# The causal mask of an LSTM moved from a minimum on VectorE into PSUM products, in a kernel of four attention and expert layers

## The chip, the cores and the metric

The kernel runs on one core of one Trainium2 chip. The metric is the device time of one execution in microseconds (us), the median over several executions. Engines are named as in the profile: PE is TensorE (matrix products; PEld its weight loads), DVE is VectorE, ACT is ScalarE, POOL is GpSimd, and SP is SyncE, which here only issues transfers. PSUM is the memory into which PE writes its results; the kernel divides it into eight banks of 128 x 512 floats. All data is 32-bit float.

## The reference

Eight sequences of 128 tokens of width 128 run through four layers; each is a kind of attention or recurrence followed by a feed-forward stage with routed experts:

```python
x = x + _L0_xattn_ref(_layernorm(x), ctx, ...)          # attention, heads mixed before and after softmax
x = x + _L0_ffn_ref(_layernorm(x), ...)                 # 8 experts, top 2
x = x + _L1_xattn_ref(_layernorm(x), ctx, ctx, ...)     # the LSTM: 8 heads of 16
x = x + _L1_ffn_ref(_layernorm(x), ...)                 # self-attention, then 8 experts, top 1
x = x + _L2_xattn_ref(...); x = x + _L2_ffn_ref(...)    # cross-attention; 8 experts, top 2, one shared
x = x + _L3_xattn_ref(...); x = x + _L3_ffn_ref(...)    # cross-attention; 7 experts, top 1, one shared
```

The change concerns the LSTM of layer 1, whose heads are computed in matrix form:

```python
log_fg = jax.nn.log_sigmoid(fg)
cs = concatenate([zeros((1, 1)), cumsum(log_fg, axis=0)], axis=0)
log_fg_matrix = jnp.where(ltr, (cs - cs.T)[1:, 1:], -jnp.inf)    # ltr: lower triangle
log_D = log_fg_matrix + ig.T
max_log_D = jnp.max(log_D, axis=-1, keepdims=True)
D = jnp.exp(log_D - max_log_D)
C = q @ (k.T / sqrt(DH)) * D
normalizer = jnp.maximum(jnp.abs(C.sum(-1, keepdims=True)), jnp.exp(-max_log_D))
return C / (normalizer + EPS) @ v
```

## The kernel before

**Recording and planning.** The program isn't written in the order in which it runs. The layers are walked through with recording engines (`Noting`, `Engine`): each call makes an operation in a `Plan`, with what it reads and writes. `Plan.schedule` (line 317) then places all 3556 operations on the engines by estimated durations of its own, gives every tile a buffer out of a fixed number for each size (`SLOTS`, line 106; PSUM's eight banks are the class `ps`), and `emit` issues the calls in the order found. Every instruction recorded in this way has the same line in the profile, 486, so groups are told apart by their tiles' names: `ps` is PSUM, `f` a buffer of 1024 columns, `d` of 512, `k` of 256, `h` of 128, `s` of 16, `cst` the constants.

Which operation goes first where several are ready is decided by a due time (`ranks`, line 297): the PE time recorded ahead of the operation in its lane, less the length of the chain that hangs on it, plus a number out of the list `MOVED` (one for each twelve operations in the order of recording, 297 of them). The sequences are treated in two halves of four, each half a lane; lane 1 begins `LAG` later than lane 0 (80e3 ns). An operation that two engines can do (`either`, `on_sbuf`) goes where the plan has it done first: copies out of PSUM on ACT or DVE, elementwise work on SBUF on DVE or POOL.

**The layers.** `first` to `fourth` (lines 1697 to 1728) are walked for each half in turn. Each ends with experts: `route` picks a token's experts and scatters its row into a table in DRAM (`routed_z`); `table` counts the rows of each expert (one product, `cnt`); `run` loads the rows back, transposes them (`zp`), takes the up and down products and stores the results (`routed_y`); the next layer's `combine` gathers these, adds them to the sequence, normalizes and goes on. So each half has, at each layer, two passages through DRAM in which it can't go on, and the other half's work is to fill PE meanwhile.

**The LSTM.** `second` (line 1706) combines layer 0's experts, enters each sequence, and computes the gates of four sequences together (`gates`, line 1474): products for the forget gate (`fp`) and the input gate (`ip`), logarithms and exponentials on ACT, running sums and maxima on DVE, out of which come two arrays `a` and `g`, made so that one product over the 32 rows of a pair of heads gives log D minus its maximum. `self.done` is the last operation of that. Then `heads` (line 1515) is called for each sequence, followed by that sequence's self-attention (`m1`):

- `gm` and `qm` (names `k` in the profile) are made from `g` and the normalized input, on DVE or POOL.
- Eight products over 32 rows each (lines 1530 to 1539) put log D for two heads into columns 0 to 255 of four banks, and q times k into columns 256 to 511.
- On DVE, for each bank, a minimum with the constant `causal` (0 on and below the diagonal of a sequence, -1e30 above it) goes into the SBUF tile `dm` (an `f` buffer), and ACT takes the exponential there, in place (lines 1541 to 1546).
- On DVE, a multiply with the bank's other 256 columns (line 1548).
- Eight products with the values, of 32 columns each (`lav`), a copy, three transposes (`hp`), and the normalizer on DVE and POOL.

A record of PE is one pass: a product of floats makes two records, a transpose one. `plan.gate(op)` (line 229) makes the next operation wait for `op`; `cut()` ends a group of products that are placed together.

Of the kernel before, what the change touches and what calls it, by code (L numbers as in the profile page):

```python
# [14 lines left out]
AF = mybir.ActivationFunctionType  # L15
ALU = mybir.AluOpType
# [59 lines left out]
TURN, START = 93.0, 20.0  # L76
WIRE, LANDED = 290.0, 1350.0
QUEUED = 3700.0
LAG, TAIL = 80e3, 1.0
WEIGHT = {"DVE": 2.0, "ACT": 1.0, "POOL": 1.0}  # L80

TWELVE = 12
MOVED = [
    -1083, -1103, 205, -26, 57, -1175, -1600, -534, 34, -1891, -1239, -1364, -627, -3743,
    -3852, -3408, -603, -286, 235, -1161, 144, -256, 89, -549, -189, -1327, -3092, 41, -483,
    141, -137, -208, -1657, -152, -932, -2161, -2352, -3148, -3024, -2046, -1584, -3502,
    -5867, -1561, -1719, -125, -35, -250, -563, -188, -355, -215, 323, 839, 446, -81, -67,
    -47, 334, 122, 86, -324, 369, 291, -2385, -631, -411, -389, 462, 551, 633, 36, -1330, 187,
    -94, 126, 885, 2267, 2293, 1164, 721, 298, 429, 830, -217, 343, -1869, -623, -2263, -2314,
    -2361, -2571, -2185, -2458, 410, 730, -870, -2137, -615, -230, -384, 1568, 492, 212,  # L90
    -1062, 420, -250, -172, 191, 825, 1849, 456, 1310, -1102, 1348, 1994, -369, -1270, -1096,
    -1627, 75, 108, -498, 90, 936, 32, 25, 1018, 3277, 726, -1256, 3162, -2159, -3746, -1331,
    -490, -407, 130, -1177, 9, 932, 115, 119, -1157, 64, -116, -1259, 80, 3, -316, -1507, -4,
    354, -263, 104, 1161, -594, -1648, -2533, 257, -731, 60, 678, 770, 1063, 81, -220, -934,
    798, 1927, -2080, -2719, -606, 103, 475, -861, -1176, -203, 698, 1199, -4415, -2711,
    -2001, -1291, -638, -375, 1467, -850, 140, -426, 526, -13, -482, -612, -549, 1735, -687,
    -388, -248, 485, -1085, 327, -196, -1695, -57, -534, -652, -881, -1067, 89, 309, 906,
    -1478, -1495, 772, -1075, 279, -312, -853, -1024, -1330, -810, -2709, -4, -804, -2785,
    -2274, -1909, 332, 647, -382, 1390, -41, 1307, -3, -902, 646, 2147, 1652, 2969, 2877,
    1837, 27, 71, -806, -885, 555, -375, 475, 942, 642, 1341, 1623, 428, -1195, -892, -4739,  # L100
    -2152, -1436, 145, 342, -2013, 977, -73, 240, 425, 357, 1504, 1022, -397, 2304, 6399,
    4433, 2665, 3535, 204, 3623, 2833, 183, 277, -25, 2797, -319, 149, 1919, 1192, 2590, 2033,
    1396, -190, 414, 358, 1190, -2626, -2536, -1306, 295,
]
ENGINES = ("PE", "DVE", "ACT", "POOL", "SP")
SLOTS = {
# [87 lines left out]
class Plan:  # L194
# [39 lines left out]
    def cut(self):  # L234
        self.run = None
# [368 lines left out]
def blocks(ctx: ExitStack, tc: tile.TileContext, t: dict, out: bass.AP):  # L604
    nc = tc.nc
# [7 lines left out]
    plan = Plan(nc)  # L613
# [14 lines left out]
    real, nc = nc, Noting(plan, nc)  # L628

    def bank(name):  # L630
        return plan.tile([P, 512], name, "ps")
# [34 lines left out]
    ident = cst[:, C_ID : C_ID + P]  # L666
    tri = cst[:, C_TRI : C_TRI + P]
    causal = cst[:, C_CAUS : C_CAUS + P]
# [34 lines left out]
    cut = plan.cut  # L703
# [24 lines left out]
    def on_sbuf(op, *args):  # L728

        either((nc.vector, op, args, {}), (nc.gpsimd, op, args, {}))  # L730


    def mm(dst, w, src, start=True, stop=True):
        nc.tensor.matmul(dst, lhsT=w, rhs=src, start=start, stop=stop)


    def on_axis(idx):
        return bass.IndirectOffsetOnAxis(ap=idx.now(), axis=0)

    def scatter(dst, idx, src, last=None):  # L740

        kw = {} if last is None else {"bounds_check": last, "oob_is_err": False}

        def call():
            real.gpsimd.indirect_dma_start(  # L745
                out=dst.ap, out_offset=on_axis(idx), in_=src.now(), in_offset=None, **kw
            )

        plan.add("POOL", call, [dst], [idx, src], 1050.0, (1300.0, 65536))

    def gather(dst, src, idx):
        def call():
# [75 lines left out]
    class Routed:  # L828
# [25 lines left out]
        def route(self, b, src):  # L854
# [46 lines left out]
            for k in range(top):  # L901
                scatter(self.views[at + k], idx[:, j, k : k + 1], z)
# [553 lines left out]
    class Lstm:  # L1456
# [58 lines left out]
        def heads(self, b):  # L1515
            j = b % HB
            part = slice(j * P, (j + 1) * P)
            full = [P, 2, P]
            cvz = T([P, 8, 32], f"cvz_{b}")
            plan.gate(self.done)  # L1520
            nc.sync.dma_start(out=cvz, in_=t["cvz"][b])
            gm = T(full, f"gm_{b}")
            qm = T(full, f"lq_{b}")
            for dst, src, sel in ((gm, self.g, gate2), (qm, self.zT, head2)):
                on_sbuf(
                    "tensor_tensor", dst, src[:, part].unsqueeze(1).to_broadcast(full),
                    sel.unsqueeze(2).to_broadcast(full), ALU.mult,
                )
            cut()
            es = [bank(f"e_{b}_{r}") for r in range(4)]  # L1530
            for k, (l, m) in enumerate(
                ((self.a[:, part], gm), (ctxT[:, b * P : (b + 1) * P], qm))
            ):
                for r in range(4):
                    rows = slice(r * 32, r * 32 + 32)
                    mm(
                        es[r][:, k * 256 : (k + 1) * 256], l[rows, :],
                        m[rows].rearrange("p h s -> p (h s)"),
                    )
            dm = T([P, 4, 2, P], f"dm_{b}")  # L1540
            for r in range(4):
                nc.vector.tensor_tensor(
                    dm[:, r], es[r][:, :256].rearrange("p (h s) -> p h s", h=2),
                    causal.unsqueeze(1).to_broadcast(full), ALU.min,
                )
                nc.scalar.activation(dm[:, r], dm[:, r], AF.Exp)
            for r in range(4):
                nc.vector.scalar_tensor_tensor(
                    dm[:, r].rearrange("p h s -> p (h s)"), es[r][:, 256:512], 0.25,
                    dm[:, r].rearrange("p h s -> p (h s)"), ALU.mult, ALU.mult,  # L1550
                )
            cut()
            av = bank(f"lav_{b}")
            for n in range(2):
                for i in range(4):
                    h = n * 4 + i
                    mm(
                        av[i * 32 : i * 32 + 32, n * P : (n + 1) * P], cvz[:, h, :],
                        dm[:, h // 2, h % 2, :],
                    )  # L1560
            hT = T([P, 2 * P], f"hT_{b}")
            copy(hT, av[:, : 2 * P])
            cut()
            hp = bank(f"hp_{b}")
            for n in range(2):
                nc.tensor.transpose(
                    hp[:, n * P : (n + 1) * P], hT[:, n * P : (n + 1) * P], ident
                )
            nc.tensor.transpose(hp[:, 2 * P : 3 * P], self.em[:, part], ident)

            hs = T([P, 3 * P], f"hs_{b}")
            copy(hs, hp[:, : 3 * P])
            cut()
            h3 = hs[:, : 2 * P].rearrange("p (h c) -> p h c", c=32)
            e3 = hs[:, 2 * P :].rearrange("p (r c) -> p r c", c=32)[:, :, 0:4:2]

            def t8(what):
                return T([P, 8], f"{what}_{b}")

            nrm, ms, w = t8("nrm"), t8("ms"), t8("lw")  # L1580
            nc.vector.scalar_tensor_tensor(
                nrm, h3[:, :, 16], -1.0, h3[:, :, 16], ALU.mult, ALU.max
            )
            nc.vector.tensor_tensor(
                nrm.rearrange("p (r c) -> p r c", c=2), nrm.rearrange("p (r c) -> p r c", c=2),
                e3, ALU.max,
            )
            nc.vector.tensor_scalar(nrm, nrm, 1e-6, None, ALU.add)
            nc.vector.scalar_tensor_tensor(nrm, nrm, 1e-6, nrm, ALU.mult, ALU.mult)
            sq = T([P, 8, 16], f"sq_{b}")  # L1590
            on_sbuf("tensor_tensor", sq, h3[:, :, 0:16], h3[:, :, 0:16], ALU.mult)
            cut()
            nc.vector.tensor_reduce(ms, sq, AX.X, ALU.add)
            nc.vector.scalar_tensor_tensor(ms, ms, 1.0 / 16.0, nrm, ALU.mult, ALU.add)
            nc.gpsimd.tensor_tensor(w, ms, nhalf, ALU.pow)
            cut()
            hv = T([P, 8, 16], f"hv_{b}")
            on_sbuf(
                "tensor_tensor", hv, h3[:, :, 0:16], w.unsqueeze(2).to_broadcast([P, 8, 16]), ALU.mult
            )  # L1600
            on_sbuf("tensor_tensor", x[b], hv.rearrange("p h d -> p (h d)"), x[b], ALU.add)
# [328 lines left out]
```

## Time and profile before

| | |
|---|---|
| median of 9 runs | 661.31 us (659.34 to 665.52) |
| the profiled execution | 664.96 us; span of its instructions 663.2 us |
| granted TensorE clock, mean | 0.937 |
| PE idle, 663.2 - 589.0 | 74.2 us |
| LSTM of half 0: `fp` to the last `hp` | 182.6 to 226 us |
| LSTM of half 1: `fp` to the first head's sums | 273.2 to 289.2 us |
| the minima with `causal` on DVE | 32, mean 413 ns |
| the exponentials after them on ACT | 32, mean 418 ns |
| the multiplies after these on DVE | 32, mean 411 ns |

Durations and stretches come from one execution, taken by the hardware profiler. A busy share is an average over stages, so a change is to be read in its own stage: which wait ends last there. A group of the profile gives the busy time, the mean of one instruction, and the time for which its engine was idle before such instructions, with what ended that. The granted clock is the share of its full speed at which PE was let run; where it is 0.5, each product takes twice as long.

### The profile page before, as it was taken

What the parts mean: (1) busy time and instruction counts of PE and PEld (TensorE: products, weight loads), DVE (VectorE), ACT (ScalarE), POOL (GpSimd) and SP (SyncE); (2) the same over time, 40 slices, a digit from 0 to 9 for tenths busy, and PEclk for the clock granted to TensorE, in tenths of its full rate; (3) what the DMA queues carried; (4) which work ended last, traced back from release to release, by engine and by line L of the source; (5) the groups of instructions that cost most, each with busy time, mean ns of one, the idle gap of its engine ahead of it and who ended that gap; (6) DMA issues with size and microseconds to landing.
All of it is one profiled execution on the core that took longest, in us unless ns stands there. A gap on an engine that the chain in (4) does not pass through costs nothing.

```text
span 663.2 us, 14423 instructions
## 1 busy us (share of the span) xinstructions
PE 589.0 (89%) x5082; PEld 473.1 (71%) x5082; DVE 421.1 (64%) x1353; ACT 328.9 (50%) x888; POOL 328.0 (49%) x475
## 2 busy tenths in 40 slices
PE   5999999999869887869997999989898989888995
PEld 5787678778647674447875778878576976665995
DVE  2055455453687877488975869547686658766464
ACT  5776665674544542537763467434343432352211
POOL 6134435312876477435586745162676028722434
PEclk9999999999998998858997999989798998796999
DMA  7999500694005826004016037642502851012581
GB/s 270 316 288 321 146 1 17 175 293 149 25 24 157 279 81 267 22 9 138 18 37 267 6 108 254 191 161 81 196 5 85 297 176 41 24 52 69 181 327 73
DMA packets 87618, 93.26 MB, mean 141 GB/s; under 512 B 6283, under 2 KB 72309, under 8 KB 87162
## 3 DMA queue, kind: packets, MB, share of 16 engines
q1 hardware_dynamic: 83338, 84.68, 39.4%
q0 software_dynamic: 3776, 6.84, 3.2%
q8 instruction: 40, 0.66, 0.4%
q10 hardware_dynamic: 432, 0.83, 0.3%
q14 instruction: 32, 0.26, 0.1%
HBM read 62.74 MB, written 30.49 MB: 141 GB/s over the span
## 4 chain that ended last, share of the span: by engine, by line
PE 55%; DVE 14%; DMA 11%; POOL 9%; issue 6%; ACT 4%; SPq 0%; POOLq 0%; DVEq 0%; ACTq 0%
PE ps L486 55%; DMA h<-routed_y,u 4%; DVE d L486 4%; DVE nmp L486 4%; POOL s L486 3%; DVE s L486 2%; DVE f L486 2%; POOL routed_z L745 2%; DMA g<-in_f 2%; ACT g L486 1%; POOL d L486 1%; DVE h L486 1%; DMA d<-routed_z 1%; ACT d L486 1%; POOL h L753 1%
## 5 line engine op out<-in xcount | busy, mean ns | idle before, releaser
L486 ACT ACTIVATE d<-ps 128x512 f32<-128x512 f32 (+4 forms) x120 | 62.1, 519 | 103.2 <-PE ps L486 93.9
L486 ACT COPY d<-ps 128x512 f32<-128x512 f32 (+2 forms) x157 | 80.2, 530 | 47.6 <-PE ps L486 45.3
L486 PE MATMUL ps<-d,g 128*128 128x128 f32 (+1 forms) x608 | 89.7, 303 | 1.8 <-ACT d L486 1.4
L486 PEld LDWEIGHTS ps<-d,g 128*128 128x128 f32 x608 | 74.6, 195 | 12.3 <-issue 8.8
L486 PE MATMUL ps<-d,k 32*128 32x256 f32 x768 | 65.4, 435 | 9.3 <-DVE d L486 5.9
L745 POOL DMA_INDIRECT routed_z<-h,u x48 | 51.3, 1069 | 44.6 <-DVE s L486 31.3
L486 ACT ACTIVATE g<-ps 128x512 f32<-128x512 f32 x100 | 54.3, 622 | 37.9 <-PE ps L486 36.8
L486 POOL TENSOR_TENSOR s<-s,nhalf 128x1 f32<-128x1 f32 (+1 forms) x88 | 59.9, 685 | 16.6 <-DVE s L486 13.7
L486 DVE TENSOR_REDUCE nmp<-ps 128x4 f32<-128x512 f32 x96 | 61.0, 681 | 7.8 <-PE ps L486 7.4
L486 DVE SCALAR_TENSOR_TENSOR d<-d,ps 128x512 f32<-128x512 f32 (+4 forms) x58 | 38.7, 667 | 41.9 <-ACT d L486 38.7
L486 PE MATMUL ps<-g,d 128*128 128x128 f32 (+1 forms) x432 | 56.7, 278 | 5.3 <-DVE s L486 3.5
L486 DVE TENSOR_TENSOR d<-ps,d 128x512 f32<-128x512 f32 (+4 forms) x82 | 55.2, 675 | 8.9 <-PE ps L486 4.8
L486 POOL TENSOR_TENSOR d<-d,s 128x512 f32<-128x512 f32 x26 | 26.9, 1039 | 62.9 <-DVE s L486 47.8
L486 PEld LDWEIGHTS ps<-g,d 128*128 128x128 f32 (+1 forms) x432 | 51.9, 191 | 8.1 <-issue 3.7
L486 PEld LDWEIGHTS ps<-d,k 32*128 32x128 f32 x768 | 41.4, 202 | 20.4 <-DVE d L486 7.1
L753 POOL DMA_INDIRECT h<-routed_y,u x40 | 40.1, 1003 | 26.7 <-DMA routed_y<-d 16.2
L486 ACT ACTIVATE d<-ps,s 128x128 f32<-128x128 f32 x128 | 45.7, 372 | 14.5 <-DVE s L486 13.0
L486 PE MATMUL ps<-d,f 128*128 128x128 f32 (+1 forms) x268 | 44.5, 317 | 2.0 <-DMA f<-in_f 2.0
L486 POOL TENSOR_TENSOR d<-k,cst 128x512 f32<-128x512 f32 x34 | 35.2, 1044 | 21.1 <-ACT k L486 20.5
L486 DVE TENSOR_REDUCE s<-ps 128x4 f32<-128x512 f32 x32 | 21.9, 688 | 34.8 <-PE ps L486 34.4
L486 PE MATMUL ps<-cst,h 128*128 128x128 f32 x96 | 28.2, 318 | 17.7 <-DVE h L486 13.5
L486 PEld LDWEIGHTS ps<-d,f 128*128 128x128 f32 x268 | 34.4, 199 | 6.9 <-issue 3.3
(160 smaller groups left out, 1234.0 us busy)
## 6 DMA issues: line engine op xcount, KB each, us to landing
g<-in_f SPq DMA_DIRECT2D x16, 768.0 KB
g<-in_f SPq DMA_DIRECT2D x16, 512.0 KB
g<-in_f SPq DMA_DIRECT2D x16, 384.0 KB
f<-in_f SPq DMA_DIRECT2D x16, 384.0 KB
routed_z<-zero SPq DMA_DIRECT2D x2, 2560.0 KB
routed_y<-zero SPq DMA_DIRECT2D x2, 2560.0 KB
g<-in_f SPq DMA_DIRECT2D x16, 320.0 KB
routed_x<-zero SPq DMA_DIRECT2D x8, 585.0 KB
```

The lines of the kernel that those rows point to most:

```text
L486: return getattr(real, op)(*[now(a) for a in args], **{k: now(v) for k, v in kw.items()})
L745: real.gpsimd.indirect_dma_start(out=dst.ap, out_offset=on_axis(idx), in_=src.now(), in_offset=None, **kw)
L753: real.gpsimd.indirect_dma_start(out=dst.now(), out_offset=None, in_=src.ap, in_offset=on_axis(idx))
```

## The change

Before a head's sums, four products of the identity (128 x 128) with the constant `causal`, repeated for the two heads (256 columns), write the mask into columns 0 to 255 of the four banks. The 32-row products of `a` and `gm` are then added on top of it (they no longer start a sum of their own); those of q and k, in the other columns, start anew as before. The mask's products wait for `self.done`, not for `gm`. DVE's minimum falls away, and ACT takes the exponential from PSUM into `dm`.

The number of recorded operations falls from 3556 to 3532. The list `MOVED` is another one, with 295 numbers; `LAG` goes from 80e3 to 90e3; and the plan's estimate for the landing of a scatter goes from 1300 to 1500 ns. These three change only the order in which operations are issued and the engine of those that have a choice. PE's list has 32 products more; DVE's is 22 shorter, POOL's ten shorter, ACT's and SP's are as long as they were.

```diff
-LAG, TAIL = 80e3, 1.0
+LAG, TAIL = 90e3, 1.0
...
 MOVED = [
-    -1083, -1103, 205, -26, 57, -1175, -1600, -534, 34, -1891, -1239, -1364, -627, -3743,
+    -1206, -1212, -285, 213, 140, -718, -1582, -888, 68, -2181, -912, -2488, -679, -4488,
...
-        plan.add("POOL", call, [dst], [idx, src], 1050.0, (1300.0, 65536))
+        plan.add("POOL", call, [dst], [idx, src], 1050.0, (1500.0, 65536))
...
             es = [bank(f"e_{b}_{r}") for r in range(4)]
+            plan.gate(self.done)
+            for r in range(4):
+                mm(
+                    es[r][:, :256].rearrange("p (h s) -> p h s", h=2), ident,
+                    causal.unsqueeze(1).to_broadcast(full), stop=False,
+                )
+            cut()
             for k, (l, m) in enumerate(
                 ((self.a[:, part], gm), (ctxT[:, b * P : (b + 1) * P], qm))
             ):
                 for r in range(4):
                     rows = slice(r * 32, r * 32 + 32)
                     mm(
                         es[r][:, k * 256 : (k + 1) * 256], l[rows, :],
-                        m[rows].rearrange("p h s -> p (h s)"),
+                        m[rows].rearrange("p h s -> p (h s)"), start=k == 1,
                     )
             dm = T([P, 4, 2, P], f"dm_{b}")
             for r in range(4):
-                nc.vector.tensor_tensor(
-                    dm[:, r], es[r][:, :256].rearrange("p (h s) -> p h s", h=2),
-                    causal.unsqueeze(1).to_broadcast(full), ALU.min,
+                nc.scalar.activation(
+                    dm[:, r].rearrange("p h s -> p (h s)"), es[r][:, :256], AF.Exp
                 )
-                nc.scalar.activation(dm[:, r], dm[:, r], AF.Exp)
```

## The prediction

> **What bounds the kernel now.** I read the page's busy shares first, then the shares of the chain that ended last:
>
> ```profile
> PE 589.0 (89%) x5082; PEld 473.1 (71%) x5082; DVE 421.1 (64%) x1353; ACT 328.9 (50%) x888; POOL 328.0 (49%) x475
> ...
> PE 55%; DVE 14%; DMA 11%; POOL 9%; issue 6%; ACT 4%; SPq 0%; POOLq 0%; DVEq 0%; ACTq 0%
> ```
>
> PE is the nearest to a bound, and the change gives it work and takes work from DVE, which is idle a third of the time. What that is worth depends on where PE stands still or runs at a low clock. So next the table of stretches, cut at PE's waits (window, its length; then busy us of PE, weight load, DVE, ACT, POOL; then the granted clock, DMA share, GB/s):
>
> ```profile
> 113.60:125.30 11.70, 11.70 (x66) 7.95 (x66) 6.95 (x26) 7.09 (x25) 6.08 (x9) 1.00 0.33 97
> 184.60:198.70 14.10, 8.14 (x60) 6.69 (x58) 12.45 (x52) 6.67 (x17) 10.52 (x15) 0.95 0.08 27
> 198.70:226.00 27.30, 25.88 (x259) 20.43 (x260) 21.57 (x66) 14.44 (x37) 17.64 (x25) 0.90 0.64 182
> 226.00:276.00 50.00, 41.38 (x404) 30.89 (x403) 33.95 (x111) 20.26 (x48) 30.12 (x44) 0.90 0.46 164
> 276.00:289.20 13.20, 5.16 (x21) 3.06 (x20) 9.63 (x36) 5.37 (x7) 5.78 (x11) 0.75 0.07 20
> 289.20:303.60 14.40, 13.77 (x106) 8.97 (x106) 11.93 (x47) 5.46 (x15) 4.82 (x7) 0.52 0.34 100
> 344.50:357.70 13.20, 8.90 (x138) 6.45 (x136) 7.82 (x25) 4.90 (x13) 8.92 (x12) 1.00 0.81 302
> ```
>
> 184.6 to 198.7 is the LSTM of half 0, from its second gate product to its first head: PE idles 6.0 us. 276.0 to 303.6 is the LSTM of half 1: 8.0 us idle ahead of the first head, then four heads at a clock of 0.52, with DVE busy 11.9 of 14.4 us. These are the worst stretches, and the change lies in them. The chain of waits shows what runs there (start, length, what), and the timeline what PE waited for (in brackets):
>
> ```profile
> 198.02 0.64 POOL k L486
> 198.70 2.13 PE ps L486 x16
> 200.83 4.38 DVE f L486 x13
> ```
>
> ```profile
> 198.70 1.24 PE L486 MATMUL ps<-k,d 32*128 32x256 f32 x8 [5.93 <-POOL k L486]
> ...
> 280.41 0.33 PE L486 MATMUL ps<-cst,h 128*128 128x128 f32 x1 [2.43 <-DVE h L486]
> ```
>
> "DVE f" is a head's minima and multiplies: once the sums are in PSUM, DVE sets the pace.
>
> **The products added.** The trace has no 128-row product of 256 columns; its neighbours, as records of two passes to a product:
>
> ```profile
> 39.65 1.02 PE L486 MATMUL ps<-d,h 128*128 128x512 f32 x2
> 40.51 0.60 PE L486 MATMUL ps<-cst,d 128*128 128x128 f32 x4
> 40.95 1.06 PE L486 MATMUL ps<-ctxT,g 128*128 128x128 f32 x8
> 41.84 1.02 PE L486 MATMUL ps<-d,h 128*128 128x512 f32 x2
> ```
>
> Start to start, one product of 512 columns takes 40.51 - 39.65 = 0.86 us, and four of 128 take 41.84 - 40.95 = 0.89, or 0.22 each. Half of 0.86 is 0.43 for 256 columns, which I take: 8 heads x 4 x 0.43 = 13.8 us at full clock. The ends are 32 x 0.22 = 7.1 and 32 x 0.86 = 27.5. Some of it is hidden. The first set of half 0 stands right ahead of sums that waited 5.93 us, so its 1.7 us are free. In the new order little else stands between the four heads of half 0 (17 us of PE work in all, of which the sets are 6.9), so PE would wait there for exponentials and multiplies; of the other three sets (5.2 us) I count 3 as hidden. Half 1's sets stand among expert products and pay in full. So 13.8 - 4.8 = **+9.0 us**; with the cover gone, +13.8.
>
> **The minima removed.** 32 of 413 ns, in the groups by shape (busy us and mean ns, then idle time before them and what ended it):
>
> ```profile
> L486 ACT ACTIVATE f<-f 128x256 f32<-128x256 f32 x32 | 11.7, 418 | 18.0 <-DVE f L486 18.0
> L486 DVE TENSOR_TENSOR f<-ps,cst 128x256 f32<-128x256 f32 x32 | 11.6, 413 | 4.2 <-PE ps L486 4.2
> ...
> L486 ACT ACTIVATE d<-ps 128x256 f32<-128x256 f32 x14 | 5.4, 384 | 15.2 <-PE ps L486 15.2
> ```
>
> That is 13.2 us off DVE. On the chain, DVE's f pieces between 200 and 294 us that exceed 0.7 us sum to 4.38 + 1.09 + 2.33 + 1.59 + 0.74 = 10.1 us; half of these instructions are minima, so about 5 us of chain go: **-5 us**. Next late are the exponential (0.42 us, which waited for DVE 18.0 us in all) and the multiplies. The other end is 0, if those or POOL's k (198.02, above) set the heads anyway. DVE gets work in turn: its list is only 22 shorter, since ten small operations come over from POOL, and it takes five copies of 128x512 (0.69 us each) from ACT. That is some 6 us, spread over a DVE that is 64% busy; I cost it at nothing, and at up to 3 us where DVE is the pace, inside the range. The exponential now reads PSUM: by the last row and the first 384 against 418 ns, 1.1 us off an ACT that is half idle, and where it has a bias operand (484 ns, the group into k) 2.1 us more: nothing either way.
>
> **The order.** A list of due times is replaced, so all engines' orders differ. I set PE's two orders beside each other and priced the work that stands between an operation and the one that must wait for what follows from it, with the rows above (0.11 for a transpose, 0.54 for four 32-row products). The list sums to 509 us before and 523 after; what counts is the cover of each latency.
> Gains:
> - second gate product to first head, half 0: cover 5.5 to 10.5, where PE idled 6.0: -5.0.
> - half 1: before, 1.4 us of cover and 8.7 us idle from 276.0 to 303.6. After, layer 1's experts of half 0 come ahead of the first head: 10.2 us of dense work. But these wait for their rows: routing's count ran at 291.2, the load was issued at 297.1, and such a load took 3.35 on the chain (at 212.79), so 9.3 us with 3.6 of cover, 5.7 idle. -3.0.
> - clock: 5.16 x 0.25 + 13.77 x 0.48 = 7.9 us were lost to it from 276.0 to 303.6. The same heads among dense expert products (306 to 316 ran them at 1.00) should win back 6, as the wait of 5.7 may cost some. Ends 0 and 7.9. -6.0.
> - last down product of layer 1 to the next attention: 7.1 to 10.8, where 4.3 were idle: -3.7. Two smaller ones (156 and 542 us): -1.9.
> - half 1's first experts move some 9 us of work into the stretch 226 to 276, which had 8.6 idle; I take half, -4.3.
>
> Losses, at a need of 9.3 us for a routing:
> - layer 0, half 0: 11.2 to 7.6, +1.7. Layer 1, half 1: 7.6 to 5.5, +2.1. Layer 2, half 0: 12.4 to 5.4, +3.9. Last layer: 6.9 to 3.4, +3.5. Layer 0, half 1, to its LSTM: 10.8 to 7.9, +2.9. Together +14.1, up to 20.
>
> SP's and POOL's queues are reordered with the rest; POOL's list is ten shorter, and an SP load moved ahead of its need costs only where it delays another, which these covers hold.
> Order: -23.9 + 14.1 = **-9.8 us**. Switches between tile shapes fall from 181 to 173, worth under a microsecond.
>
> **The sum.** 9.0 - 5 - 9.8 = -5.8 us. The profiled execution took 664.96 (span 663.2, 1.8 around it), 3.65 over the median of 661.31; -5.8 gives 659.2 for such an execution and 655.5, say **656**, for the median. About 0.5% (3.3 us) is what a measurement can tell from no change.
>
> [...] From 276.0 to 303.6 the clock was 0.75 and 0.52, though PE's longest gap there is 2.43 us (280.41, above). [...]
>
> **Rivals.**
> - Slower: the hole ahead of the experts. For it: after the 5.93 us of idle at 198.7 the clock fell (0.90 from 198.7 to 226, the 0.95 before it). If 5.7 us of waiting in half 1 does the same, the 6 us of clock aren't won and half of the 10.2 us of expert work behind it runs at half clock, 5 us: 656 + 11 = 667. It decides once that stretch has a clock under 0.7 with PE idle over 5 us. Against it: expert work is dense and lifts the clock again.
> - No change: five of the eight sets are followed at once by their sums, so none runs ahead as meant, and the hidden 4.8 us are paid: 656 + 5 = 661. The same time comes if the minima were not the pace (0 for 5). For it: POOL's k ended the longest wait.
> - Faster by more: the five covers lost are half as dear as I count, since the old ones were more than full (113.6 to 125.3 had no idle at all): 656 - 7 = 649.
>
> **Chances.** Slower by the hole or by covers dearer than counted 0.38; no change 0.16; my forecast 0.36 and the greater gain 0.10, so faster 0.46. The likeliest case alone reaches from 650 to 660. For 8 in 10 the low end goes past the greater gain to 646 and the high end past the hole to 670, where the products at 0.86 us would also put it (656 + 13.7).
>
> **What would show it.** PE's new group should have 64 records, start to start 0.21; PE idle before the first head of half 0 should fall from 6 to about 1 us; the heads of half 1 should run at a clock over 0.8; no exponential should wait for DVE f. The prediction is wrong if PE's idle time in routing (the last layers above all) grows by much over 14 us, or the clock over the span falls below 0.937.

## The result, and the profile after

| | us, median | range, runs | ratio to before |
|---|---|---|---|
| kernel before | 661.26 | 656.29 to 668.42, 62 | |
| changed kernel | 675.42 | 670.06 to 680.39, 20 | 1.0204, 95% interval 1.0183 to 1.0224 |

The changed kernel is 2.0% slower, 14 us. 656 was forecast, with 646 to 670 as the range; the kernel became slower, not faster.

The profiled execution of the changed kernel took 670.4 us (span 668.6, granted clock 0.956), 5 us under its median. The difference is clock: span times clock is 639.2 us there and 638 to 641 in its other runs (675.0 at 0.949, 671.3 at 0.954). The profiled execution of before (664.96) lay 3.7 over its median. So the two traces are only 5.4 us apart where the medians are 14.2 apart, and the shares below show the changed kernel somewhat too well.

From the page of the changed kernel, the busy shares and the chain that ended last:

```profile
PE 590.9 (88%) x5146; PEld 477.0 (71%) x5146; DVE 419.9 (63%) x1331; ACT 326.3 (49%) x888; POOL 318.1 (48%) x465
...
PE 50%; POOL 14%; DVE 14%; DMA 9%; issue 7%; ACT 5%; SPq 0%; POOLq 0%; DVEq 0%; ACTq 0%
```

DVE's busy time fell by 1.2 us though the minima, 11.6 us busy as a group, are gone: it got some 10 us of other work. PE's part of the chain shrank from 55 to 50% and POOL's grew from 9 to 14%.

The stretches that answer to those shown of before (window, its length; busy us of PE, weight load, DVE, ACT, POOL; granted clock, DMA share, GB/s):

```profile
111.20:120.20 9.00, 7.88 (x65) 7.17 (x64) 4.25 (x20) 5.55 (x21) 3.84 (x4) 1.00 0.24 68
145.80:167.50 21.70, 18.18 (x80) 11.83 (x80) 11.02 (x28) 10.63 (x46) 11.74 (x14) 0.92 0.70 207
185.70:197.90 12.20, 12.20 (x95) 10.77 (x94) 9.18 (x33) 7.17 (x19) 6.24 (x11) 1.00 0.03 12
277.70:348.30 70.60, 55.57 (x408) 43.54 (x409) 43.54 (x129) 36.17 (x82) 29.24 (x43) 0.80 0.17 53
278.70:295.80 17.10, 10.20 (x25) 5.87 (x26) 7.19 (x39) 2.40 (x6) 10.22 (x17) 0.50 0.17 49
309.50:316.30 6.80, 5.80 (x20) 4.62 (x24) 4.52 (x7) 3.99 (x9) 3.77 (x4) 0.50 0.00 0
606.80:613.40 6.60, 5.28 (x12) 2.14 (x11) 4.48 (x15) 1.19 (x2) 0.96 (x1) 0.77 0.24 72
```

185.7 to 197.9 is the LSTM of half 0 up to its first head: PE is busy throughout, as forecast. 277.7 to 348.3 is the LSTM of half 1 with layer 1's experts of half 0 among its heads: clock 0.80, and 17 and 7 us of it at 0.50. The same piece of before; the first part of that, from its first transposes to its gate products; and, third row, the way of before from the last down product of layer 0 to the first LSTM:

```profile
265.90:327.80 61.90, 50.57 (x445) 37.97 (x444) 48.95 (x157) 36.02 (x82) 28.48 (x45) 0.81 0.16 50
265.90:276.20 10.30, 9.98 (x104) 6.40 (x103) 5.70 (x22) 5.41 (x14) 5.04 (x10) 0.85 0.05 15
156.50:170.80 14.30, 13.26 (x81) 9.59 (x79) 7.50 (x28) 7.94 (x30) 7.65 (x10) 1.00 0.30 78
```

So the clock of the second LSTM was not won (0.81 to 0.80), its PE idle time rose from 11.3 to 15.0 us, and the way to the first LSTM takes 21.7 us in place of 14.3.

The new products and the exponentials, groups by shape (busy us and mean ns; idle before them and what ended it):

```profile
L486 PE MATMUL ps<-cst 128*128 128x256 f32 x64 | 17.0, 413 | 0.0
L486 ACT ACTIVATE f<-ps 128x256 f32<-128x256 f32 x32 | 9.9, 388 | 9.5 <-PE ps L486 9.5
```

64 records, and no exponential waits for DVE any more. From the start to PE's last record, PE's idle time (no record of PE or of its weight load) is 73.0 us against 67.5.

### The profile page after: what moved, and what is told of

It reads as the page before. It is cut to its first block, busy times and chain, and to the rows that moved or that the text cites. A ratio compares the mean times of both kernels' runs of the same rounds, so it can differ in the third digit from the quotient of the medians.

```text
span 668.6 us, 14522 instructions
## 1 busy us (share of the span) xinstructions
PE 590.9 (88%) x5146; PEld 477.0 (71%) x5146; DVE 419.9 (63%) x1331; ACT 326.3 (49%) x888; POOL 318.1 (48%) x465
## 4 chain that ended last, share of the span: by engine, by line
PE 50%; POOL 14%; DVE 14%; DMA 9%; issue 7%; ACT 5%; SPq 0%; POOLq 0%; DVEq 0%; ACTq 0%
PE ps L486 50%; DVE d L486 5%; POOL s L486 4%; DMA h<-routed_y,u 4%; DVE s L486 3%; POOL routed_z L745 3%; POOL h L753 3%; DMA d<-routed_z 2%; DVE nmp L486 2%; ACT d L486 2%; POOL d L486 2%; ACT g L486 2%; POOL h L486 2%; DVE x L486 1%; DVE h L486 1%
## 5 line engine op out<-in xcount | busy, mean ns | idle before, releaser
L486 ACT ACTIVATE d<-ps 128x512 f32<-128x512 f32 (+3 forms) x125 | 63.3, 509 | 108.1 <-PE ps L486 103.9
L486 ACT COPY d<-ps 128x512 f32<-128x512 f32 (+2 forms) x150 | 76.9, 531 | 69.3 <-PE ps L486 62.4
L486 DVE TENSOR_REDUCE nmp<-ps 128x4 f32<-128x512 f32 x96 | 60.9, 683 | 13.8 <-PE ps L486 13.8
L486 PE MATMUL ps<-d,k 32*128 32x256 f32 x768 | 57.4, 406 | 7.1 <-DVE d L486 3.7
L486 DVE TENSOR_TENSOR d<-ps,d 128x512 f32<-128x512 f32 (+2 forms) x82 | 55.3, 674 | 7.5 <-PE ps L486 3.1
L486 POOL TENSOR_TENSOR d<-d,s 128x512 f32<-128x512 f32 x28 | 29.0, 1039 | 60.4 <-DVE s L486 59.3
L753 POOL DMA_INDIRECT h<-routed_y,u x40 | 39.6, 989 | 31.9 <-issue 19.4
L486 ACT ACTIVATE d<-ps,s 128x128 f32<-128x128 f32 x128 | 45.5, 371 | 13.5 <-DVE s L486 13.3
L486 PEld LDWEIGHTS ps<-d,k 32*128 32x128 f32 x768 | 38.6, 189 | 16.3 <-DVE d L486 5.3
L486 PE MATMUL ps<-cst,d 128*128 128x128 f32 x232 | 36.6, 280 | 8.9 <-DMA d<-routed_z 5.2
L486 POOL TENSOR_SCALAR s<-s 128x1 f32<-128x1 f32 x42 | 9.9, 239 | 68.0 <-DVE s L486 65.5
L486 PEld LDWEIGHTS ps<-cst,d 128*128 128x128 f32 x232 | 27.4, 143 | 20.6 <-issue 10.7
```

Source lines behind the costliest of these rows:

```text
L486: return getattr(real, op)(*[now(a) for a in args], **{k: now(v) for k, v in kw.items()})
L753: real.gpsimd.indirect_dma_start(out=dst.now(), out_offset=None, in_=src.ap, in_offset=on_axis(idx))
```

## The experiments

Ratios are to the kernel before, run beside them on the same chip, with 95% intervals. What was expected of each run stands ahead of its result; the diffs are shortened. In the first two sets the kernel before took 675 us, in the last three 662 to 663; more on that at the end.

**Parts against order.** "Old order" is each engine's order in the kernel before, "new order" that of the changed kernel. The parts are exchanged within one order: a minimum is issued right ahead of its exponential, a set of products right ahead of its sums.

```diff
+    sums.ways[0][1][here] = masks               # old order: four products, then the sums
+    least.ways[0][1][0] = lambda: None          # old order, no minima
+    exp.ways[0][1][0] = lambda r=r: nc.scalar.real.activation(dm_r, es_r, AF.Exp)
...
+    exp.ways[0][1][0] = least                   # new order: minimum, then exponential
+    plan.run.ways[0][1][-4:] = [lambda: None] * 4   # new order, no products
```

> The kernel before with its own order on every engine; each head's four products with the identity stand right ahead of its sums, the exponential reads PSUM, the 32 minima are gone. By the terms of my prediction: 661 + 13.8 (nothing of the products is hidden where the sums follow at once) - 5 (minima) = 670, and less what the first set of each half hides in a wait, 1.7 x 2: about 666. Theory 'the products are paid': the products are the whole loss of 14 and the minima were worth nothing: 675. Theory 'the new order lost it': products and minima about cancel, 661 to 665.

> The kernel before with its own order, the four products ahead of each head's sums, and the minima kept behind them (they change nothing then): what the products cost by themselves. By the prediction's terms 661 + 13.8 - 3.4 = 671; this run less the one without minima is what the minima were worth, 5. Theory 'the products are paid': 675, and no difference between the two. Theory 'the new order lost it': under 668.

> The changed kernel's order on every engine, without the products; each minimum stands right ahead of its exponential, as in the kernel before. What the order does by itself. By the prediction's terms 661 - 9.8 = 651. Theory 'the products are paid': 661, no difference from the kernel before. Theory 'the new order lost it': 670 to 675, slower by 1.5 to 2%, with PE's idle time in the routings grown as it has in the changed kernel.

> The changed kernel with the minima put back ahead of the exponentials, the products kept. Less the changed kernel (675.4) this is what the minima cost in the new order; less the run of the new order with minima alone it is what the products cost there. By the prediction's terms +5 and +9: 680 and 671 for that other run. Theory 'the products are paid': 675 (minima nothing), products 14. Theory 'the new order lost it': products under 5.

| order | products | minima | ratio |
|---|---|---|---|
| old | yes | no | 0.9983 (0.9945 to 1.0021) |
| old | yes | yes | 1.0060 (1.0030 to 1.0089) |
| new | no | yes | 1.0414 (1.0373 to 1.0454) |
| new | yes | yes | 1.0354 (1.0306 to 1.0402) |

In the old order the products cost 0.6%, 4 us, and the minima were worth 0.8%, 5 us: the change of parts alone makes no difference. In the new order it is slow with either part, so the order loses; with the products it is no slower than without them. (There, a minimum at its exponential's place may stand badly on DVE; 1.041 is not the price of the order alone.)

**The same chip for both orders, and the price of a product.** The products are also made in 16-bit floats, one pass in place of two (32 records in the trace in place of 64), and the order is worked out anew from the old due times.

```diff
+    half = K([P, 384], "half", bfloat16)      # identity and mask, copied once
-    mm(es[r][:, :256], ident, causal2, stop=False)
+    mm(es[r][:, :256], half_ident, half_causal2, stop=False)
 # and, in another kernel: the changed one with
-LAG, MOVED and the scatter's 1500.0 of the changed kernel
+LAG, MOVED and the scatter's 1300.0 of the kernel before
```

> The changed kernel once more, unchanged, on the chip of the three runs beside it, because the kernel before took 661 us on one chip and 675 on another. Theory 'the order lost it': about 1.02 times the kernel before again, with PE idle for some 73 us against 65 in the old order with products. Rival 'it was the chip': within 0.5% of the old order with products (0.998).

> The old order with products and without minima, as before (0.998 of the kernel before), but the 32 products take a copy of the identity and of the mask in 16-bit floats, so that each should be one pass over 256 columns in place of two. What a product costs the kernel. If the products are paid in full: one pass of 0.11 to 0.21 us in place of 0.43 saves 32 x 0.22 to 0.32 = 7 to 10 us, 0.983 to 0.988 of the kernel before. Rival 'they stand where PE would wait or be slowed anyway' (the difference with and without them was only 4 us): under 3 us, 0.994 to 0.998.

> The changed kernel's order with the same 16-bit products. If the products are paid in full: 7 to 10 us less than the changed kernel, 1.005 to 1.010 of the kernel before. If the new order waits elsewhere around its heads: under 3 us less, 1.016 to 1.020.

> The changed kernel with the list of due times, the lag between the halves and the scatter's price of the kernel before: the order is worked out anew around the products, but from the old list. Theory 'the new list lost it': near the old order with products, 0.998 to 1.006. Rival 'any order worked out around products that stand ahead loses, as it holds four banks of PSUM early': 1.015 or more, with PE's idle time over 72 us.

The changed kernel came to 1.0362 (1.0299 to 1.0425) here: the order again, not the chip. Half products: 0.9974 (0.9941 to 1.0007) in the old order, 1.0306 (1.0226 to 1.0385) in the new. From the timeline of the old order with half products and then of that with full ones (start, length, what; the wait ahead of it in brackets):

```profile
192.96 0.49 PE L1555 MATMUL ps<-half 128*128 128x256 bf16 x3
...
199.06 1.24 PE L486 MATMUL ps<-k,d 32*128 32x256 f32 x8 [4.60 <-POOL k L486]
```

```profile
193.01 1.93 PE L1546 MATMUL ps<-cst 128*128 128x256 f32 x8
199.11 0.71 PE L486 MATMUL ps<-k,d 32*128 32x256 f32 x8 [4.18 <-POOL k L486]
```

A half product takes 0.11 us ((0.49 - 0.27) / 2, with 0.27 for the last one's length), a full one 0.43 to 0.46 (start to start in the changed kernel: 1.73 us for the four at 335.83, 1.83 for those at 197.94), and the sums start at 199.1 either way, when POOL's k is there. Some 10 us less of products (32 x 0.32) are worth nothing that can be measured: the rival was right. Planning anew from the old list gave 1.0578 (1.0526 to 1.0631): the theory that the new list is what lost fell, since for these operations the new list is far better than the old one. The number fits the rival of that run, that products which stand ahead hold four banks of PSUM early; whether that is its reason was not tested. In the changed kernel's trace the eight sets begin 1.8 to 3.6 us ahead of their sums.

**Where in the order.** All operations are the changed kernel's; a table gives every engine the one order up to a point and what is left in the other. The buffers are given out along that table.

```diff
-    plan.schedule(plan.ranks())
+    plan.replay()    # first part: order X up to the point; then order Y
```

> All operations of the changed kernel (products, no minima). Until the first attention of the third layer (m2) every engine follows the order of the kernel before, with each set of products right ahead of its sums; what is left then follows the changed kernel's order. Where in the order the loss lies. Counted at equal progress of PE's records, the changed kernel's idle time and half of its time at half clock (runs on chips where the kernel before takes 675) come to 76 us at half of the records against 47 in the old order with products, and to 51 against 63 in the second half. Theory 'the first half of the new order loses': 0.998 less 12 us, 0.980 of the kernel before. Rival 'the loss is spread over the order': 1.017.

> The mirror of it: the changed kernel's order until the first attention of the third layer, then the order of the kernel before. Theory 'the first half of the new order loses': 0.998 and 29 us, 1.041. Rival 'spread': 1.017.

> The changed kernel's order until the LSTM of the first half begins, then the order of the kernel before. Up to there the changed kernel had 21 us of idle time and clock loss against 7, most of it in one wait of 3.5 us at 158 and in the clock behind it. If that place loses by itself: 1.015 to 1.02. Rival 'the loss comes behind it, in the LSTM of the second half': 0.995 to 1.002.

> The order of the kernel before until the LSTM of the second half begins, then the changed kernel's order. From there to half of PE's records the changed kernel had 41 us of idle time and clock loss against 18. Theory 'the LSTM of the second half among layer 1's experts loses': 23 more and 12 less, 1.012 to 1.018. Rival 'what loses lies ahead of it': 0.980 to 0.988, like the old order up to the third layer.

| first, then | ratio |
|---|---|
| old until the third layer, then new | 1.0010 (0.9970 to 1.0049) |
| new until the third layer, then old | 1.0301 (1.0246 to 1.0357) |
| new until the LSTM of half 0, then old | 1.0202 (1.0147 to 1.0256) |
| old until the LSTM of half 1, then new | 1.0113 (1.0075 to 1.0152) |

The changed kernel itself has 1.015 to 1.020 on this kind of chip, and two ways lead to it from the old order. From the back: with the new order behind the third layer 1.0010; with the way from the second LSTM to there new as well 1.0113, 6.8 us more; with all of it new, another 3 to 6 us. From the front: with the new order ahead of the first LSTM 1.0202, 14.5 us more than 0.9983 (which is from the other kind of chip); up to the third layer 1.0301, 6.6 us more; with all of it new, 6 to 10 us less.

The two ways agree on one place: the new order loses about 7 us from the second LSTM to the third layer, whichever order stands around it (the 6.6 holds the stretch between the two LSTMs too). They don't agree on the rest, so the losses of the places do not simply add up. The way to the first LSTM costs 14.5 us when the old order follows, but it and the stretch between the LSTMs together only 3 to 6 us when the new one does. Behind the third layer the new order costs 2 us after the old one and gives back 6 to 10 us after the new one. Each of these differences is uncertain by some 4 to 5 us. My 0.980 for the best mixture did not come, and 1.0301 lies between what theory and rival had.

Worked out from these profiles, PE's idle time plus half of its time at half clock, in us, when so many of PE's records have started (one trace each, and equal counts of records aren't quite equal work; the kernel before has some 14 us less of products to do):

```
                                        20%    35%    50%   100%
before                                  7.5   32.4   62.5  108.5
changed kernel                         16.1   27.4   65.0  102.0
new until the LSTM of half 0, old      19.7   38.8   56.9   97.4
old until the LSTM of half 1, new       7.7   28.6   68.2  105.7
old until the third layer, new          7.5   27.5   46.2   92.0
```

The new order loses 9 to 12 us before 20%. Where it goes on, it has won that back by 35%: from 20 to 35% the changed kernel loses 11.3 us (13 to 14 in two more traces of it), the old order 20 to 21. Where the old order follows, nothing is won back (19.1). Between 35 and 50% the new order loses some 20 us more than the old one (37.6 and 39.6 against 18.7 and 18.1); of these, 8 come back behind that, where the last two rows have the same order (37.5 against 45.8). So what the changed kernel pays in the end stands between the second LSTM and the third layer: by the times the larger part (7 us against 3 to 6), by this count nearly all.

**What loses ahead of the first LSTM.** This is the place that costs most where the old order follows. The longest wait there in the changed kernel is 3.5 us, from 158.7 on, for a softmax's multiply. DVE's timeline at that place:

```profile
157.15 0.35 DVE L486 SCALAR_TENSOR_TENSOR x<-h,s,x 128x128 f32<-128x128 f32 x1 [1.65 <-DMA h<-routed_y,u]
157.42 0.68 DVE L486 TENSOR_REDUCE s<-ps 128x4 f32<-128x512 f32 x1
159.35 0.35 DVE L486 SCALAR_TENSOR_TENSOR x<-h,s,x 128x128 f32<-128x128 f32 x1 [1.25 <-DMA h<-routed_y,u]
159.61 0.17 DVE L486 RECIPROCAL s<-s 128x4 f32<-128x4 f32 x1
159.73 0.29 DVE L486 BATCH_NORM_STATS2 s<-x 128x6 f32<-128x128 f32 x1
161.01 0.35 DVE L486 SCALAR_TENSOR_TENSOR x<-h,s,x 128x128 f32<-128x128 f32 x1 [0.99 <-DMA h<-routed_y,u]
161.28 0.18 DVE L486 BATCH_NORM_AGGREGATE s<-s 128x2 f32<-128x6 f32 x1
161.38 0.66 DVE L486 TENSOR_TENSOR d<-d,s 128x512 f32<-128x512 f32 x1
```

The reciprocal (159.61) and the multiply (161.38) had their operands from 156.2 on, when ACT's last exponential for them ended, but stood behind sums that wait for gathered expert results (x<-h,s,x). That looks like the cause, so it was taken away; and all three queues were sorted by readiness, in both orders.

```diff
+    late = [plan.ops[i] for i in (979, 980, 981, 1012, 982)]   # sums into x, statistics
+    rest = [op for op in plan.order if op not in late]
+    at = rest.index(plan.ops[726]) + 1                         # the softmax's multiply
+    plan.order = rest[:at] + late + rest[at:]
...
-    plan.schedule(plan.ranks())
+    plan.replay()    # sorted: PE and SP as they were, DVE, ACT and POOL by readiness
```

> The changed kernel unchanged, as the measure of the next two on the same chip: 1.02 where the kernel before takes 661, 1.036 where it takes 675.

> The changed kernel with five small DVE instructions put behind two others: the sums of two gathered expert results into x (each waits for its gather) and their statistics come behind the reciprocal and the multiply of the second half's softmax, which were ready at 156.2 but started at 159.6 and 161.4 in the changed kernel. Theory 'DVE's queue': PE's wait of 3.5 us at 158.7 falls under 0.7, and the kernel is 2 to 4 us (0.3 to 0.6%) faster than the changed kernel beside it. Rival 'the cover is gone, whatever the queue': a wait of over 2 us stays at that softmax or comes back within 10 us, and the time is within 0.3%.

> The changed kernel with PE's and SP's order as they are; on DVE, ACT and POOL an instruction that is ready by the measured durations goes ahead of one that still waits (some 350 of 2,500 move up). Theory 'the queues of these three engines are the loss of the new order': 1.000 to 1.006 of the kernel before. Rival 'the loss lies in PE's own order, which leaves short chains uncovered': within 1% of the changed kernel beside it, and its distance to the old order sorted in the same way stays over 1.5%.

> The old order with products (0.998 of the kernel before), its three queues sorted in the same way. If instructions that wait at the head of a queue cost PE time in any order: 0.985 to 0.992. If measured readiness does not carry over to a changed order: 0.998 to 1.005.

Changed kernel 1.0151 (1.0090 to 1.0212), softmax first 1.0185 (1.0118 to 1.0252), sorted 1.0611 (1.0544 to 1.0678), the old order sorted 1.0401 (1.0340 to 1.0461). Sorting makes both orders 4% slower, which none of the expectations had. It leaves their distance at 2.1%, over the rival's 1.5, but says nothing on the queues of the tuned order. Softmax first: the multiply went at 156.60, and PE then waited 6.06 us at 159.7 until DVE's copy out of PSUM at 165.03, which still stood behind such a sum. So the copy, another reciprocal and a second softmax's two instructions were put ahead as well:

```diff
-    x sums and statistics (9) among reciprocals, multiplies and a copy (7)
+    the 7 first, then the 9; no other engine's order changes
```

> The changed kernel unchanged, as the measure of the run beside it: 1.015 to 1.02 where the kernel before takes 661, 1.036 where it takes 675, with PE's wait of 3.5 us at 158 to 162.

> The changed kernel with nine small DVE instructions (four sums of gathered expert results into x, one more of x1, and their statistics) put behind seven that were ready and stood after or among them: reciprocals and multiplies of two softmaxes, and the copy that frees the PSUM bank for which PE waited in the run before, where only the first softmax had been moved. Nothing else changes. Theory 'DVE's queue': no wait of PE over 1 us between 155 and 168, and 3 to 5 us (0.4 to 0.8%) off the changed kernel beside it. Rival 'the cover is gone, whatever the queue': waits of over 2 us in sum between 155 and 175, and within 0.3% of the changed kernel.

Changed kernel 1.0162 (1.0119 to 1.0206), with them first 1.0224 (1.0178 to 1.0269). PE's timeline of the latter:

```profile
159.33 0.60 PE L486 MATMUL ps<-cst,d 128*128 128x128 f32 x4
159.76 1.02 PE L486 MATMUL ps<-d,h 128*128 128x512 f32 x2
160.62 1.06 PE L486 MATMUL ps<-d,d 128*128 128x128 f32 x8
166.58 0.30 PE L486 MATMUL ps<-cst,h 128*128 128x128 f32 x1 [4.90 <-DVE h L486]
168.18 0.47 PE L486 MATMUL ps<-cst,h 128*128 128x128 f32 x1 [1.30 <-POOL h L486]
```

The softmaxes no longer wait, and now PE stands for 6.2 us at the next thing in its own order, the LSTM's first transposes, whose rows have to come through gather, sum, statistics and POOL's power. The wait moves; it does not go, and neither move made the kernel faster (0.3 and 0.6% slower than the changed kernel beside it, with intervals that overlap). So these instructions at the head of DVE's queue are not what costs. Nor did PE's work shrink: between the last down product of layer 0 (145.8) and the LSTM PE has 18.2 us of it, against 13.3 before, but the chain that it has to cover takes 21.7 us in place of 14.3.

The rows at 157 to 161 show DVE keeping the order it was given: the multiply had its operands from 156.2 on and started at 161.38, behind the sums; with the sums put behind it, it started at 156.60. That run shows too that a block at the head of DVE's queue need not be what costs: 1.0185, with 1.0151 for the changed kernel beside it.

Why the chain itself is longer (145.8 to 167.5 against 156.5 to 170.8) is open. Of its eight gathers the traces have the landing of three in the changed kernel, 3.9 to 5.1 us after issue, and of two before, 2.6 us; and four zero fills of routing buffers are issued at 150 to 157, while the kernel before issues such fills at 125 to 129 and then from 201 on. Whether the fills delay the gathers was not tried.

## Why the prediction was wrong

**Where the 14 us come from.** By the medians and ratios, the parts alone are -1 us (0.9983) on the chips where the kernel before takes 675. On the others the nearest run is 1.0010: all products in the old order's places, only the order behind the third layer new. The rest is the order: +9 to +13 us by the latter (1.015 to 1.020 less 1.0010), +11 to +15 by the former, and 26 us on the slower chips alone (1.0362 less 0.9983). Forecast were +4.0 for the parts and -9.8 for the order. The step that failed is **the order**, and in it above all the way from the second LSTM to the third layer: -12.7 us forecast, +6.8 measured.

**The products, +9.0.** The duration was right: 0.43 us forecast, (199.77 - 197.94) / 4 = 0.46 in the changed kernel's trace:

```profile
197.94 1.89 PE L486 MATMUL ps<-cst 128*128 128x256 f32 x8
199.77 0.71 PE L486 MATMUL ps<-k,d 32*128 32x256 f32 x8
```

That half 0's first set is free was right too. But even right ahead of their sums, where I would have hidden almost nothing, they cost 4 us of 13.8 in the old order, and half products cost no less. The hidden part was sized too small by 5 us. For the first set the rows at 193 and 199 show why, the sums wait for POOL's k anyway; for half 1's sets the clock is a likely reason (below). Together with the next term, -1 us was measured where +4.0 was forecast.

**The minima, -5.** Right: 0.7 to 0.8%, 5 us, in the old order. In the new order they are worth nothing that shows (1.0354 with them, 1.0362 without, on two chips of one kind). No exponential waits for DVE, and reading PSUM made it 388 in place of 418 ns. The work that came to DVE was some 10 us and not 6; that it comes for nothing was not tested by itself.

**The order, -9.8.** By place, the terms I wrote down against what the mixtures of the two orders show:

| place | terms | forecast | measured |
|---|---|---|---|
| up to the first LSTM | routing +1.7, half of "two smaller" -1.0 | +0.7 | +14.5 if the old order follows |
| from there to the second LSTM | -5.0, -4.3, +2.9 | -6.4 | with the row above +3 to +6 if the new order follows |
| second LSTM to third layer | -3.0, clock -6.0, -3.7 | -12.7 | +6.8 |
| behind that | +2.1, +3.9, +3.5, -0.9 | +8.6 | +2 after the old order, -6 to -10 after the new one |

(By the need of 9.3 us that I had set, the loss ahead of half 1's LSTM, +2.9, should have been 9.3 - 7.9 = +1.4. The eight switches between tile shapes that fell away are 0.8 us: in the changed kernel eight 128x128 products take 0.99 us start to start right behind products of another tile shape, 332.25 to 333.24, and 0.89 among their own, 150.18 to 151.07.)

At the waits that I had listed, the direction was mostly right. Ahead of the first head of half 0 PE's idle time went from 6.0 to 0.0, ahead of that of half 1 from 8.0 to 3.8. Of the waits for a routing's rows, those of the first and last layer grew by a third to two thirds of what I had counted (1.2 and 1.3 us, rows 111.20 and 606.80), and that of layer 2 stayed as it was (1.2 against 1.3 us): the covers were more than full, as the rival "faster by more" said.

What failed is the method: I priced cover only where the old order had waited, and from PE's list alone. The new order waits in other places: 25 waits of over 1 us against 19 in the traces, among them 3.5 us at 158.7, where I had counted a gain. The second LSTM shows it best. I priced the cover between its gate products and its first head. But the other work that had stood among its transposes and gate products was gone: PE was busy for 9.98 of 10.30 us there before (row 265.90:276.20), and in the changed kernel for 10.20 of 17.10 (row 278.70). Of these 6.9 us of waiting the sum had at most the +2.9 for half 1's way to its LSTM. The run that takes only the order from the second LSTM on from the changed kernel has such waits there too and, further on, ahead of the experts' down products:

```profile
282.50 0.33 PE L603 MATMUL ps<-cst,h 128*128 128x128 f32 x1 [1.17 <-POOL h L603]
290.86 0.48 PE L603 MATMUL ps<-cst,h 128*128 128x128 f32 x1 [1.93 <-DVE h L603]
308.49 1.16 PE L603 MATMUL ps<-g,d 128*128 128x128 f32 x8 [2.00 <-DVE d L603]
311.26 2.07 PE L603 MATMUL ps<-g,d 128*128 128x128 f32 x8 [1.61 <-DVE d L603]
```

No list of old waits shows such places; the chain behind each operation that was moved has to be followed.

None of the signs that I had named for being wrong came: the waits for routed rows grew by some 2.5 us and not by 14, and the clock over the span was above 0.937. The signs for being right all came. They were all local, and the loss stood elsewhere.

**The clock, -6.0.** Where it was priced it was not won: from the second LSTM's first transposes to its last head 0.81 became 0.80. The heads ran faster, as forecast (0.88 from 312.4 to 348.3), but the low clock went over to the transposes and gate products ahead of the experts (0.50 from 278.7 to 295.8) and to the experts' down products with the first set (0.50 from 309.5 to 316.3, where a product of that set takes (315.92 - 312.37) / 4 = 0.89 us). Over the span the clock did rise, 0.937 to 0.956 in the traces, but in other stretches, and PE's idle time with it.

The old order with the products did win clock there. The row of before's stretch, in the run with the old order up to the third layer:

```profile
265.90:327.80 61.90, 53.03 (x483) 40.41 (x479) 43.78 (x145) 35.00 (x81) 30.53 (x48) 0.88 0.15 50
```

0.88 in place of 0.81: the half clock around half 1's first heads lasted 10.2 us (283.6 to 293.8) in place of 20.5 (282.7 to 303.2). At half clock 10 us more would be worth some 5 us, which would account for most of what I had not counted as hidden of half 1's sets. There is one trace of before to compare with, so this is likely and not shown.

**Waits and the clock.** In the half-clock stretch from 278.7 to 295.8 PE's waits are 2.17 us at most. Some of them, from its start on:

```profile
277.66 0.33 PE L486 MATMUL ps<-cst,h 128*128 128x128 f32 x1 [0.97 <-DVE h L486]
280.38 0.48 PE L486 MATMUL ps<-cst,h 128*128 128x128 f32 x1 [2.17 <-POOL h L486]
281.41 0.59 PE L486 MATMUL ps<-wsm,d 128*128 128x8 f32 x2 [0.55 <-ACT d L486]
283.55 0.47 PE L486 MATMUL ps<-cst,h 128*128 128x128 f32 x1 [1.24 <-POOL h L486]
```

The stretch of before has 2.43 us at most (276.0 to 303.6). This one ran at 0.50 and that one at 0.75 and then 0.52, so the lower clock did not come with a longer wait. Here PE was busy for 10.2 of 17.1 us, in short pieces.

**The rivals.** "The hole ahead of the experts" (667) has its sign, a clock under 0.7 with PE idle over 5 us (0.50 and 6.9 us from 278.7 to 295.8). But the wait came in pieces, at the LSTM's transposes and gates, and not as one wait for the experts' rows; and of the experts' work only the down products, from 309.5 on, ran at half clock. The up products, right behind the stretch at 0.50, ran at 1.00 (295.8 to 306.4, PE busy for 9.73 of 10.60 us). "No change" (661) is what the parts alone do, for another reason than the one given. No rival had the loss on the way to the first LSTM.

## What to carry to other kernels

When a change comes with a new order, separate the two before explaining anything: the old order with the new parts and mixtures of both orders showed what no reading of the lists did. Mix from the front and from the back: here the two ways gave one place the same price and another 14.5 us or 3 to 6, and only what both show holds for the kernel itself. Cover counted at the old waits gives the gains of a new order and none of its losses; follow the chain behind each piece of work that moves earlier, for that is where PE will stand next. Work put into a stretch that waits or runs at a low clock anyway can cost far less than its own time (4 of 13.8 us here), and making it three quarters cheaper can then be worth nothing.

## What was not expected of the hardware

The same kernel before took 661 to 663 us on some chips and 675 on two others, the changed kernel 672 to 675 and 698; the mean record of the 256 of `ps<-ctxT,g` is 276 ns on both kinds (kernel before, and old order with products on a slower chip). The new order costs more on the slower chips, 3.6% over the kernel before against 1.5 to 2.0%. In the trace of the changed kernel from one of the slower chips ACT's copy of an attention result begins at 528.33, 3.8 us after PE's last record before it has ended (524.18 and 0.33 long), with nothing else ahead of it on ACT. PE's timeline there:

```profile
524.18 0.33 PE L486 MATMUL ps<-cst,h 128*128 128x128 f32 x1
528.75 0.47 PE L486 MATMUL ps<-cst,k 128*128 128x128 f32 x1 [4.25 <-ACT k L486]
```

On the first chip the same copy follows PE within 0.1 us. What the engine waits for there no view shows; it stays open.
